# Dividing the last three block products of a Strassen-Winograd MLP layer once more

## The chip, the cores and the metric

The kernel runs on one core of a Trainium2 chip. The metric is the device time of one execution in microseconds. Before the change it was 453.57 us, the median of three runs (452.7 to 453.67).

## The reference

The input is 32 sequences of 128 tokens with 512 features, in float32. A conditional block works on it as 8 long sequences of 1024 tokens: a first residual branch (an MLP from 512 to 512 features in two directions, on masked tokens alone), and a second one, an MLP from 512 to 1024 and back to 512 on all tokens. The change touches the second branch only. Cut to that:

```python
ff_ada = silu(t) @ ffada_w + ffada_b
shift_mlp, scale_mlp, gate_mlp = split(ff_ada, 3)
ff_norm = layernorm(x) * (1 + scale_mlp) + shift_mlp
h = gelu(ff_norm @ ff_w1 + ff_b1)          # 512 -> 1024, tanh form
out = x + gate_mlp * (h @ ff_w2 + ff_b2)   # 1024 -> 512
```

## The kernel before, in words

The second branch goes over the 4096 tokens in four rounds, called pairs (p = 0 to 3). A pair holds 8 sequences of 128 tokens, 4 on each of two sides. Both layers are computed by Winograd's form of Strassen's method: a matrix product is divided into 2 x 2 blocks, and 7 block products P1 to P7 take the place of 8. With S1 to S4 the four sums of blocks of the left operand (S1 = a21 + a22, S2 = S1 - a11, S3 = a11 - a21, S4 = a12 - S2), the products are P1 = a11 b11, P2 = a12 b21, P3 = S4 b22, P4 = a22 T4, P5 = S1 T1, P6 = S2 T2, P7 = S3 T3, with T1 to T4 four such differences of the weights. The result's blocks are P1 + P2 (block 11), P1 + P6 + P5 + P3 (12), P1 + P6 + P7 + P4 (21) and P1 + P6 + P7 + P5 (22).

**The first layer** (class FirstProduct) is divided twice: seven streams of seven inner products. Its matmuls have line 1123, and its results are the two hidden tiles ha and hb of the pair. The streams run in pairs ("windows"); while one window's products run on TensorE, VectorE and GpSimd add what its results need (on VectorE lines 1148, 1153, 1167 and the sums of the next streams' tokens, `token_sums`, lines 1051 to 1061; on GpSimd lines 1174, 1203, 1207), and ScalarE copies results out of PSUM (L1181) or applies gelu.

**The second layer** (class SecondProduct) is divided once, for two halves of the pair's tokens, U (c = 0) and V (c = 1), apart. A block product is 8 matmul calls (2 tiles of 128 tokens by 4 of features) of 256 columns each, all at line 1310; the profile has two records for a call. Each token half has two PSUM banks, e and a, that products are added onto one after the other: P5, P2, P3 onto e; P1, P6, P7, P4 onto a. The order is a list, and steps of the list carry further work ("fills") that is issued behind them:

```python
ORDER = "P1U P5U P1V P5V P2U P6U P2V P6V P3U P7U P3V P7V P4U P4V".split()
```

What stands behind a product: after P5, ScalarE keeps e as `p5` (L1016) and VectorE makes S2; after P2, VectorE multiplies block 11 with the gate, adds it to the residual x (`finish`, lines 1284 and 1286), and makes the fourth block in place in ha's second half; after P6, e becomes a + p5 (L1334), to which P3 is added; after P3 block 12 is finished; after P7 block 22 is made (L1340) and finished; after P4 block 21, and the side is stored. The third block is made in place in hb's first half (L1274).

**The next pair** is prepared by fills: its rows are normalised (L934) and turned on VectorE (L1481), carried into feature rows by DMAs, scaled and shifted by ScalarE (`scaled`, 16 activations a side, L944), and cut into blocks by four sums of 1024 elements on VectorE (`TokenBlocks.one`, L991, called `begin` 1 to 4). Then the next pair's first stream's products P5, P1 stand behind step 11 (P7V), P2 and P6 behind step 12 (P4U) of the list, and the sums of weights for its streams are loaded on the SyncE queue (`load_weights`, L1069, tile tw). In pair 0 the second layer's T1 to T4 are made as well (`combine`, by VectorE). In the last pair P4V is split in two halves that are finished apart (L1324). A window of the first layer follows: the next pair's (stream 2) P5 and P1, (stream 1) P3 and P7, (stream 2) P2 and so on; the seed of a stream's e bank for stream 2 is line 1167, that of P3 of stream 1 is line 1148.

Of the kernel before, what the change touches and what calls it, by code (L numbers as in the profile page):

```python
# [22 lines left out]
def kernel(  # L23
# [883 lines left out]
    ORDER = "P1U P5U P1V P5V P2U P6U P2V P6V P3U P7U P3V P7V P4U P4V".split()  # L907
# [64 lines left out]
    class TokenBlocks:  # L972


        def __init__(self, p, xT):
            hk = KC // 2
            self.xa, self.xb = xT
            self.s12 = sp.tile([P, 2 * hk, G * S], F32, tag="s12", name=f"s12_{p}")
            self.s4 = sp.tile([P, hk, G * S], F32, tag="s4", name=f"s4_{p}")
# [4 lines left out]
        def one(self, j):  # L984
            out, x, y, op = {
# [245 lines left out]
    class SecondProduct:  # L1231


        def __init__(self, p, h, xs):
            self.p, self.xs = p, xs
            self.ha, self.hb = h
            self.banks, self.p5, self.gate = {}, {}, {}
# [54 lines left out]
        def step(self, step, late=False):  # L1292
            p, ha, hb, s1, w = self.p, self.ha, self.hb, self.s1, fw2_of.of
            hh = HC // 2
            product, n = ORDER[step][:2], ORDER[step][2]
            c = "UV".index(n)
            tok = self.cols[c]
            e, a = self.banks[c]
            bank = bank_of(product, (e, a))
            src = {  # L1300
                "P1": ha[:, :hh, tok], "P2": ha[:, hh:, tok], "P3": ha[:, hh:, tok],
                "P4": hb[:, hh:, tok], "P5": s1[c], "P6": s1[c], "P7": hb[:, :hh, tok],
            }[product]
            last = p == NP - 1 and step == len(ORDER) - 1
            for i in range(2):
                part = bank[:, ts(i, D // 2)]
                if last:
                    part = ps_t.tile([P, 512], F32, tag="tr", name=f"last_{i}")[:, : D // 2]
                for k in range(hh):
                    nc.tensor.matmul(  # L1310
                        part,
                        src[:, k, ts(i, P)],
                        w[product][:, k, :],
                        start=(last and k == 0),
# [3 lines left out]
                if last:  # L1318

                    t = tp.tile([P, D // 2], F32, tag="t", name=f"t_last_{i}")  # L1320
                    gate = self.gate[1][:, 2 * c + i, : D // 2]
                    nc.vector.tensor_tensor(t, part, gate, ALU.mult)
                    xt = self.xs[1][c][:, i, : D // 2]
                    nc.vector.tensor_tensor(xt, xt, t, ALU.add)  # L1324
                    nc.sync.dma_start(out[(2 * p + 1) * G + 2 * c + i, :, : D // 2], xt)
# [3 lines left out]
            elif product == "P2":  # L1329
                self.finish(c, 0, 0, e)  # L1330

                nc.vector.tensor_tensor(ha[:, hh:, tok], ha[:, hh:, tok], s1[c], ALU.subtract)
            elif product == "P6":
                nc.vector.tensor_tensor(e, a, self.p5[c], ALU.add)  # L1334
            elif product == "P3":
                self.finish(c, 0, 1, e)
                self.store(c, 0)
            elif product == "P7":
                t = tp.tile([P, 512], F32, tag="t", name=f"c22_o{p}_{c}")
                nc.vector.tensor_tensor(t, a, self.p5[c], ALU.add)  # L1340
                self.finish(c, 1, 1, t)
                if p == NP - 1 and n == "V":
                    b = (2 * p + 1) * G + 2 * c
                    nc.sync.dma_start(
                        out[b : b + 2, :, D // 2 :].rearrange("b s d -> s b d"),
                        self.xs[1][c][:, :, D // 2 :],
                    )
                    self.finish(c, 1, 0, a)
            elif product == "P4" and not last:
                self.finish(c, 1, 0, a)  # L1350
                self.store(c, 1)
# [55 lines left out]
    gp = straight.enter_context(tc.tile_pool(name="gp", bufs=1))  # L1407
    now = FirstProduct(0, of_x[0].cut(), of_w)
# [25 lines left out]
    for p in range(NP):  # L1434
# [93 lines left out]
        fill = {5: [lambda: second.third_block(0)], 7: [lambda: second.third_block(1)]}  # L1528
# [4 lines left out]
        if p == 0:  # L1533
            put(2, fw2_of.combine, 2)
            put(6, fw2_of.combine, 3)
        if more_pairs:
# [3 lines left out]
            for k in range(KC):  # L1540
                put(4 + k // 2, lambda k: scaled(2 * (p + 1), xT[0], k), k)
                put(7 + k // 2, lambda k: scaled(2 * (p + 1) + 1, xT[1], k), k)
                if k == 1:
                    put(4, to_feature_rows, 1, nc.sync, nc.sync, nc.sync, nc.scalar)
# [6 lines left out]
            put(8, begin, 1)  # L1551
            put(9, begin, 2)
            put(9, begin, 3)
            put(10, begin, 4)
# [6 lines left out]
            put(10, next_product)  # L1561
            put(11, lambda: nxt["p"].do(1, "P5", "P1"))
            for n in range(4):
                put(11 + n // 2, lambda n: nxt["p"].token_sums(1, n), n)
            if p + 2 < NP:
                x_of[p + 2] = [[], []]
                put(11, lambda: x_of[p + 2][0].extend(load_side(p + 2, 0)))
            put(12, lambda: nxt["p"].do(1, "P2", "P6"))
            put(13, lambda: nxt["p"].load_weights(2))
# [130 lines left out]
```

## Time and profile before

| | us |
|---|---|
| median of three runs | 453.57 |
| lowest, highest | 452.7, 453.67 |
| the profiled execution: span | 451.7 |
| median less that span | 1.9 |

| engine | busy us | share of the span |
|---|---|---|
| TensorE (PE) | 444.0 | 98% |
| VectorE (DVE) | 334.5 | 74% |
| ScalarE (ACT) | 177.9 | 39% |
| GpSimd (POOL) | 158.4 | 35% |

The profile is of one execution. Its span runs from the first to the last instruction. A row of the timeline has the start of an instruction or a group in us, its duration, the engine, the line in the code, the operation, the output tile, the inputs and the shape, then how many instructions it stands for, and in brackets the idle time before it with what ended that. A row of the groups has line, engine, operation and tiles, the number of instructions, then the busy us and the mean ns of one, then the idle time before them. Numbers of buffers are left out of the tiles' names there.

### The profile page before, as it was taken

Reading aid. Unit: us, or ns where it says so; the run is one execution under the profiler, and the core shown is the slowest. Engines: PE = TensorE matmul, PEld = TensorE weight load, DVE = VectorE, ACT = ScalarE, POOL = GpSimd, SP = SyncE. Lnnn points to the kernel's source line nnn. Section 1 sums busy time; section 2 is a strip of 40 time slices with the busy share of each in tenths; the row PEclk is TensorE's granted clock in tenths of the full one; section 3 lists DMA queues with packets and bytes.
Section 4 is the critical chain, followed back from the end, with each engine's and each line's share of the span. In section 5 each row is a group of like instructions: output and inputs, shape, how many; then the busy total and the mean of one; then the engine's idle time right before and its main releaser. Section 6 shows DMA issues by size and latency. Waiting matters only on the chain.

```text
span 451.7 us, 6204 instructions
## 1 busy us (share of the span) xinstructions
PE 444.0 (98%) x2147; PEld 370.2 (82%) x2147; DVE 334.5 (74%) x573; ACT 177.9 (39%) x389; POOL 158.4 (35%) x154
## 2 busy tenths in 40 slices
PE   8999999999999999999999999999999999999995
PEld 3884675688888888888888888888888888888884
DVE  5797788877799759977895689878956885434645
ACT  3123116353651551536526415464265244642000
POOL 4211470089770000897600007977000027560000
PEclk9999999999999999999999999999999999999999
DMA  6999449857327717741396177512971534122022
GB/s 250 372 399 408 177 65 308 284 187 229 129 97 168 108 49 268 235 138 36 105 177 93 46 267 230 141 38 86 189 99 47 176 128 129 35 93 95 0 94 96
DMA packets 85440, 70.84 MB, mean 157 GB/s; under 512 B 63396, under 2 KB 64508, under 8 KB 84382
## 3 DMA queue, kind: packets, MB, share of 16 engines
q1 hardware_dynamic: 64270, 57.76, 42.3%
q0 software_dynamic: 4160, 10.54, 6.9%
q10 hardware_dynamic: 16976, 2.11, 3.9%
q8 instruction: 18, 0.29, 0.3%
q14 instruction: 16, 0.13, 0.1%
HBM read 56.71 MB, written 13.70 MB: 156 GB/s over the span
## 4 chain that ended last, share of the span: by engine, by line
PE 84%; DMA 8%; DVE 3%; issue 2%; POOL 1%; SPq 0%; POOLq 0%
PE a_o L1310 24%; PE a_m L1123 21%; PE e_o L1310 18%; PE e_m L1123 16%; DMA fw<-in_L_cond_ff_w_dram 3%; PE po_s L222 3%; DMA w<-in_L_cond_bwd_w_dram 3%; DMA x_wide<-t_s 2%; DMA x<-x_wide,slot_i 1%; DVE t L403 1%; PE last L1310 1%; PE a_m_alone L1123 1%; POOL x L819 1%; PE ptr L950 0%; PE pl_s L255 0%
## 5 line engine op out<-in xcount | busy, mean ns | idle before, releaser
L1174 POOL TENSOR_TENSOR ha<-p_m,ha 128x512 f32<-128x512 f32 x20 | 25.8, 1292 | 176.0 <-ACT ha L1181 166.1
L1310 PE MATMUL e_o<-fw,ha 128*128 128x256 f32 x256 | 57.9, 379 | 0.0
L944 ACT ACTIVATE xT<-xT,modT 128x128 f32<-128x128 f32 x112 | 44.0, 480 | 28.1 <-DMA xT<-xn 28.1
L1310 PE MATMUL a_o<-t,hb 128*128 128x256 f32 x240 | 54.1, 379 | 0.0
L1310 PEld LDWEIGHTS e_o<-fw,ha 128*128 128x128 f32 x256 | 48.6, 190 | 6.6
L1310 PEld LDWEIGHTS a_o<-t,hb 128*128 128x128 f32 x240 | 45.6, 190 | 6.2
L1085 ACT ACTIVATE hb<-hb,biasT 128x256 f32<-128x256 f32 x64 | 29.0, 500 | 28.3 <-POOL hb L1207 16.1
L1137 ACT COPY p_m<-e_m 128x512 f32<-128x512 f32 x27 | 15.8, 586 | 51.6 <-PE e_m L1123 51.6
L890 POOL DMA_INDIRECT x<-x_rows,slot_i x24 | 27.2, 1135 | 6.2 <-issue 5.4
L1174 POOL TENSOR_TENSOR hb<-p_m,hb 128x512 f32<-128x512 f32 x20 | 29.2, 1460 | 0.3
L1310 PE MATMUL a_o<-fw,ha 128*128 128x256 f32 x128 | 28.9, 379 | 0.0
L1310 PE MATMUL a_o<-t,s 128*128 128x256 f32 x128 | 28.9, 379 | 0.0
L1310 PE MATMUL e_o<-fw,s 128*128 128x256 f32 x128 | 28.9, 379 | 0.0
L222 PE MATMUL po_s<-w,h_s 128*128 128x512 f32 x64 | 28.4, 594 | 0.0
L1181 ACT COPY ha<-e_m 128x512 f32<-128x512 f32 x32 | 18.5, 579 | 24.8 <-PE e_m L1123 24.4
L1310 PEld LDWEIGHTS a_o<-fw,ha 128*128 128x128 f32 x128 | 24.3, 190 | 3.3
L1310 PEld LDWEIGHTS a_o<-t,s 128*128 128x128 f32 x128 | 24.3, 190 | 3.3
L1310 PEld LDWEIGHTS e_o<-fw,s 128*128 128x128 f32 x128 | 24.3, 190 | 3.3
L1148 DVE TENSOR_TENSOR e_m<-a_m,ha 128x512 f32<-128x512 f32 x20 | 14.0, 698 | 17.0 <-POOL ha L1174 7.6
L1085 ACT ACTIVATE ha<-e_m,biasT 128x256 f32<-128x256 f32 x48 | 20.0, 468 | 14.4 <-PE e_m L1123 14.4
L1123 PE MATMUL a_m<-xT,tw 128*128 128x256 f32 x96 | 24.7, 380 | 0.0
L1123 PE MATMUL e_m<-s,fw 128*128 128x256 f32 x92 | 23.7, 380 | 0.0
(234 smaller groups left out, 894.1 us busy)
## 6 DMA issues: line engine op xcount, KB each, us to landing
x<-in_x_dram SPq DMA_DIRECT2D x16, 512.0 KB, 5.9
tw<-t_rows SPq DMA_DIRECT2D x16, 512.0 KB, 4.3
gate<-gate_rows POOLq DMA_DIRECT2D x8, 1024.0 KB, 5.1
out_dram<-x SPq DMA_DIRECT2D x15, 512.0 KB, 4.7
tw<-t_rows SPq DMA_DIRECT2D x16, 384.0 KB, 3.9
xT<-xn SPq DMA_DIRECT2D x80, 64.0 KB, 2.7
ada_f<-in_L_cond_ffada_w_dram SPq DMA_DIRECT2D x4, 768.0 KB, 14.8
ada_a<-in_L_cond_ada_w_dram SPq DMA_DIRECT2D x4, 512.0 KB, 3.6
```

The costliest lines, as they stand in the source:

```text
L222: nc.tensor.matmul(po, h[f][:, ts(i, P)], w[:, f, :], start=(f == 0 and seeded is None), stop=(f == HC - 1), skip_group_check=seeded is no ...
L403: engine.tensor_tensor(out, x, y, ALU.subtract)
L819: nc.gpsimd.indirect_dma_start(out=raw[i // 2][:, i % 2], out_offset=None, in_=x1_wide[:slots], in_offset=bass.IndirectOffsetOnAxis(ap=slo ...
L890: nc.gpsimd.indirect_dma_start(out=xs[i // G][i % G // 2][:, i % 2], out_offset=None, in_=x1_rows, in_offset=bass.IndirectOffsetOnAxis(ap= ...
L944: nc.scalar.activation(out, src, AF.Identity, bias=shift, scale=scale)
L1085: nc.scalar.activation(dst[:, n], src[:, n], AF.Gelu_apprx_tanh, bias=biasT[:, f : f + 1])
L1123: nc.tensor.matmul(bank[:, ts(n, QT)], self.w_block(j, product)[:, ts(n, P)], self.x_block(j, product), start=(product in ("P1", "P5") and ...
L1137: nc.scalar.copy(p5, e)
L1148: nc.vector.tensor_tensor(e, a, p5, add)
L1174: nc.gpsimd.tensor_tensor(self.place(RESULT[j], c), self.p5[j], other, ALU.add)
L1181: nc.scalar.copy(self.place(RESULT[j], c), src)
L1310: nc.tensor.matmul(part, src[:, k, ts(i, P)], w[product][:, k, :], start=(last and k == 0), stop=True, skip_group_check=True,)
```

## The change

P3, P7 and P4 of the second layer are no longer 8 calls of 256 columns for each token half. Each is done for U and V together and divided once more by the same method into seven inner products p1 to p7 (class Inner): left blocks of 2 feature tiles by 256 tokens, right blocks of 2 feature tiles by 128 columns, so an inner product is 4 calls of 128 columns. The three are written A (P3), B (P7) and C (P4) below.

- *Their sums of the left operand* (512 elements a lane each): sums 1, 2 and 3 of A, B and C are on GpSimd, sum 4 on VectorE. All three share one tile (`si`) for sums 1 and 2; sum 3 and sum 4 are made in place in ha or hb.
- *Inner products apart*: p5 has a bank of its own, and p1, p6, p7 are added onto another; ScalarE copies what stands in the bank after each into a tile d (tag xn) of parts.
- *Inner products direct*: p2, p3 and p4 are added onto the banks e (A) or a (B and C) of U and V.
- *Fives and joins* on GpSimd: `with_five` adds the p5 part to a half of d (256 elements), and `join` adds the parts of one token half (512 elements) to p5 of the layer (A: d + p5 in d; B: p5 + d in p5; C: d + B's d in d).
- *On VectorE* e's seed takes A's parts in place of p5 (`seed_third`), block 22 takes p5 with B's parts, block 21 gets one more addition (`sum_of` with C's parts) for U and for V. In the last pair, V's block 21 is done in place with C's p4 in two halves (`last_quarters`).
- *The inner weights*: twelve subtractions of 256 elements on GpSimd in pair 0 (`inner_weights`), and the layer's combine(3) moves from VectorE to GpSimd.
- *Fills*: they are now named by inner products. The scaling of the next pair's second side is issued in halves behind p6A to p7B, `begin` 1 to 4 behind p7B, p4A, p1C and p6C; the next pair's P5 and P1 of the first stream behind p4B, P2 and P6 behind p3C, with the loads that stood there. P6V is split around p6A.

The core of the diff:

```diff
-    ORDER = "P1U P5U P1V P5V P2U P6U P2V P6V P3U P7U P3V P7V P4U P4V".split()
+    ORDER = "P1U P5U P1V P5V P2U P2V P6U".split()
+    INNER = ("P3", "P7", "P4")
...
+        def join(self, product, c, engine):
+            d = self.inner[product].d[:, c]
+            if product == "P3":
+                engine.tensor_tensor(d, d, self.five(c), ALU.add)
+            elif product == "P7":
+                engine.tensor_tensor(self.five(c), self.five(c), d, ALU.add)
+            else:
+                engine.tensor_tensor(d, d, self.inner["P7"].d[:, c], ALU.add)
...
+        def sum(self, j, engine):
+            (a11, a12), (a21, a22) = self.x
+            s1, s2 = self.s
+            out, x, y, op = {
+                1: (s1, a21, a22, ALU.add),
+                2: (s2, s1, a11, ALU.subtract),
+                3: (a21, a11, a21, ALU.subtract),
+                4: (a11, a12, s2, ALU.subtract),
+            }[j]
+            engine.tensor_tensor(out, x, y, op)
...
+        def apart(self, q):
...
+            nc.scalar.copy(self.d[:, c, :, ts(n, P)], view)
+
+        def with_five(self, c, engine):
+            d = self.d
+            other = d[:, 1, :, P:] if c == 0 else d[:, 1, :, :P]
+            engine.tensor_tensor(d[:, c, :, P:], d[:, c, :, P:], other, ALU.add)
...
         if p == 0:
+            put(2, inner_weights, "P7")
             put(2, fw2_of.combine, 2)
-            put(6, fw2_of.combine, 3)
+            put(3, lambda: fw2_of.combine(3, engine=nc.gpsimd))
+            put(3, inner_weights, "P3")
+            put(4, inner_weights, "P4")
...
+        put(5, sums, PA, 1, 2, 3)
...
+        run("p5A", lambda: inner[PA].apart("p5"))
+        sums(PB, 1)
+        run("p1A", lambda: inner[PA].apart("p1"))
+        sums(PA, 4, engine=nc.vector)
+        second.multiply("P6V", (0,))
+        run("p6A", lambda: inner[PA].apart("p6"))
+        inner[PA].with_five(0, nc.gpsimd)
+        second.multiply("P6V", (1,))
+        run("p7A", lambda: inner[PA].apart("p7"))
+        second.join(PA, 0, nc.gpsimd)
+        second.seed_third(0)
+        inner[PA].with_five(1, nc.gpsimd)
+        second.join(PA, 1, nc.gpsimd)
+        second.seed_third(1)
+        sums(PB, 2)
+        inner[PB].apart("p5")
+        run("p1B", lambda: inner[PB].apart("p1"))
+        sums(PB, 3)
+        sums(PB, 4, engine=nc.vector)
+        second.direct(PA, "p2")
+        run("p6B", lambda: inner[PB].apart("p6"))
+        sums(PC, 1)
+        second.direct(PA, "p3")
+        second.finish_third(0)
+        run("p7B", lambda: inner[PB].apart("p7"))
+        sums(PC, 2)
+        inner[PB].with_five(0, nc.gpsimd)
+        second.join(PB, 0, nc.gpsimd)
+        sums(PC, 3)
+        run("p4A", lambda: second.direct(PA, "p4"))
+        second.finish_third(1)
+        inner[PB].with_five(1, nc.gpsimd)
+        second.join(PB, 1, nc.gpsimd)
+        inner[PC].apart("p5")
+        run("p1C", lambda: inner[PC].apart("p1"))
+        sums(PC, 4, engine=nc.vector)
+        second.direct(PB, "p2")
+        run("p6C", lambda: inner[PC].apart("p6"))
+        inner[PC].with_five(0, nc.gpsimd)
+        second.join(PC, 0, nc.gpsimd)
+        second.direct(PB, "p3")
+        second.finish_22(0)
+        inner[PC].apart("p7")
+        inner[PC].with_five(1, nc.gpsimd)
+        second.join(PC, 1, nc.gpsimd)
+        run("p4B", lambda: second.direct(PB, "p4"))
+        second.finish_22(1)
+        run("p2C", lambda: second.direct(PC, "p2"))
+        second.direct(PC, "p3")
+        second.finish_21(0)
```

In the listings below a row has the line in the code, the instruction, the output tile, the inputs and the shape; x8 or x4 is the number of calls. A name's first number is the pair's (a bank e_o1_0 is pair 1's of U; fw2 and t_2 are the second layer's weights and their differences).

TensorE in pair 1, before: after V's P6 (row one) come U's and V's P3 and P7; the products follow one another, and the next pair's first stream (e_m2_1, a_m2_1) stands between them.

```order
L1310 MATMUL a_o1_1_1790<-t_2_314,s1_1_1505 128x256 x8
L1310 MATMUL e_o1_0_1731<-fw2_312,ha_1_1432 128x256 x8
L1310 MATMUL a_o1_0_1732<-t_2_314,hb_1_1433 128x256 x8
L1310 MATMUL e_o1_1_1789<-fw2_312,ha_1_1432 128x256 x8
L1310 MATMUL a_o1_1_1790<-t_2_314,hb_1_1433 128x256 x8
L1123 MATMUL e_m2_1_2023<-s12_2_1974,fw1_311 128x256 x2
```

TensorE in pair 1, now: the inner products of A (five_1_P3, one_1_P3) and B (five_1_P7, one_1_P7), with A's p2 and p3 direct onto U's bank e.

```order
L1453 MATMUL five_1_P3_2034<-fw2_312,si_1_2015 128x128 x4
L1453 MATMUL one_1_P3_2041<-fw2_312,ha_1_1515 128x128 x4
L1395 MATMUL a_o1_1_1887<-t_2_314,s1_1_1602 128x256 x4
L1453 MATMUL one_1_P3_2041<-t_1_313,si_1_2015 128x128 x4
L1395 MATMUL a_o1_1_1887<-t_2_314,s1_1_1602 128x256 x4
L1453 MATMUL one_1_P3_2041<-t_1_313,ha_1_1515 128x128 x4
L1453 MATMUL five_1_P7_2083<-t_2_314,si_1_2015 128x128 x4
L1453 MATMUL one_1_P7_2089<-t_2_314,hb_1_1516 128x128 x4
L1453 MATMUL e_o1_0_1828<-fw2_312,ha_1_1515 128x128 x4
L1453 MATMUL one_1_P7_2089<-inner_more_892,si_1_2015 128x128 x4
L1453 MATMUL e_o1_0_1828<-fw2_312,ha_1_1515 128x128 x4
```

Between A's p7 (the sixth row) and B's p6 (the tenth, which reads `si`) stand three inner products.

GpSimd in pair 1, before: between the loads of the gate and the next pair's first layer it has nothing.

```order
L928 TENSOR_TENSOR rstd_3_1_2082<-ve_3_1_2338,half_134 128x4
L901 DMA gate_2_0_2341<-gate_rows_699 128x2048
L901 DMA gate_2_1_2389<-gate_rows_699 128x2048
L1174 TENSOR_TENSOR ha_3_2578<-p5_m3_2_2648,ha_3_2578 128x2x256
L1174 TENSOR_TENSOR hb_3_2579<-p5_m3_2_2648,hb_3_2579 128x2x256
```

GpSimd in pair 1, now (L1444 is a sum, L1476 a `with_five`, L1324 and L1326 a `join`; xn_d is the tile d, p5_o1 is p5):

```order
L901 DMA gate_1_1_1913<-gate_rows_699 128x2048
L1444 TENSOR_TENSOR si_1_2015<-ha_1_1515 128x512
L1444 TENSOR_TENSOR si_1_2015<-si_1_2015,ha_1_1515 128x512
L1444 TENSOR_TENSOR ha_1_1515<-ha_1_1515 128x2x256
L1444 TENSOR_TENSOR si_1_2015<-hb_1_1516 128x512
L1476 TENSOR_TENSOR xn_d_1_2016<-xn_d_1_2016 128x2x128
L1324 TENSOR_TENSOR xn_d_1_2016<-xn_d_1_2016,p5_o1_0_1916 128x512
L1476 TENSOR_TENSOR xn_d_1_2016<-xn_d_1_2016 128x2x128
L1324 TENSOR_TENSOR xn_d_1_2016<-xn_d_1_2016,p5_o1_1_1958 128x512
L1444 TENSOR_TENSOR si_1_2015<-si_1_2015,hb_1_1516 128x512
L1444 TENSOR_TENSOR hb_1_1516<-hb_1_1516 128x2x256
L1444 TENSOR_TENSOR si_1_2015<-hb_1_1516 128x512
```

Sum 2 of B (the tenth row) stands behind the fives and joins of both of A's halves; ten more of these instructions follow the last row shown.

VectorE at the end of pair 1, before: from the next pair's token sums (sx_2) to the two seeds (e_m2_1 and e_m2_2); t_o and x are gate and residual of block 21.

```order
L1051 TENSOR_TENSOR sx_2_2032<-xT_2_1_1889 128x512
L1051 TENSOR_TENSOR sx_2_2032<-s4_2_1975 128x256
L1148 TENSOR_TENSOR e_m2_1_2023<-a_m2_1_2024,p5_m2_1_2027 128x512
L1284 TENSOR_TENSOR t_o1_1_10_2067<-a_o1_1_1790,gate_1_1_1816 128x512
L1286 TENSOR_TENSOR x_14_899<-x_14_899,t_o1_1_10_2067 128x2x256
L1167 TENSOR_TENSOR e_m2_2_2083<-a_m2_2_2084,ha_2_2005 128x512
```

VectorE at the end of pair 1, now:

```order
L1054 TENSOR_TENSOR sx_2_2208<-xT_2_1_1986 128x512
L1054 TENSOR_TENSOR sx_2_2208<-s4_2_2170 128x256
L1343 TENSOR_TENSOR c21_o1_0_2230<-a_o1_0_1829,xn_d_1_2016 128x512
L1287 TENSOR_TENSOR t_o1_0_10_2232<-c21_o1_0_2230,gate_1_1_1913 128x512
L1289 TENSOR_TENSOR x_12_898<-x_12_898,t_o1_0_10_2232 128x2x256
L1151 TENSOR_TENSOR e_m2_1_2199<-a_m2_1_2200,p5_m2_1_2203 128x512
L1343 TENSOR_TENSOR c21_o1_1_2246<-a_o1_1_1887,xn_d_1_2016 128x512
L1287 TENSOR_TENSOR t_o1_1_10_2248<-c21_o1_1_2246,gate_1_1_1913 128x512
L1289 TENSOR_TENSOR x_14_900<-x_14_900,t_o1_1_10_2248 128x2x256
L1170 TENSOR_TENSOR e_m2_2_2264<-a_m2_2_2265,ha_2_2172 128x512
```

U's block 21 now stands between the token sums and the first seed, each half has one addition more (c21), and that addition reads d, which GpSimd's last joins write.

More of the change, by code (lines that the diff above doesn't have):

```diff
@@ L1329, in step @@
             elif product == "P2":
[L1330 to L1346, printed above, removed]
-                    )
[L1348 to L1351, printed above, removed]
+                if c == 0:
+                    self.finish(c, 0, 0, self.banks[c][0])
```

217 lines of the change are left out of this document (172 added, 45 removed).

## The prediction

> **What bounds the kernel now.** I read the page first, then the chain of waits in order of time, the groups of instructions with shapes kept apart, and the timeline of the second pair's second product (211 to 285 us), where every engine can be followed.
>
> ```profile
> PE 444.0 (98%) x2147; PEld 370.2 (82%) x2147; DVE 334.5 (74%) x573; ACT 177.9 (39%) x389; POOL 158.4 (35%) x154
> POOL 4211470089770000897600007977000027560000
> PE 84%; DMA 8%; DVE 3%; issue 2%; POOL 1%; SPq 0%; POOLq 0%
> ```
>
> TensorE is busy for 98% of the span and makes 84% of the chain that ended last. GpSimd's row has a run of zeros in each pair: those are the second products, the stage that is changed. The chain of waits shows what one block product is worth there, and two more rows bound the last pair's stage:
>
> ```profile
> 433.21 3.45 PE e_o L1310 x16
> 412.33 3.62 PE L1310 MATMUL e_o<-fw,ha 128*128 128x256 f32 x16
> 447.52 0.43 DVE L1324 TENSOR_TENSOR x<-x,t_last 128x256 f32<-128x256 f32 x1
> ```
>
> Sixteen records (each of 8 calls is recorded twice) take 3.453 us, so a record of 256 columns costs 215.8 ns, back to back. TensorE's time is the kernel's time as long as every other engine delivers ahead of it.
>
> **What TensorE saves.** A pair loses six block products, 96 records, 20.72 us, and gets 3 x 28 calls, 168 records of 128 columns. The opening has such records:
>
> ```profile
> 16.21 3.65 PEld L681 LDWEIGHTS ph_s<-xT_s,w 128*128 128x128 f32 x32 [0.35 <-issue]
> L681 PEld LDWEIGHTS ph_s<-xT_s,w 128*128 128x128 f32 x64 | 7.3, 192 | 0.4 <-issue 0.4
> ```
>
> The 32 loads start within 3.65 - 0.19 = 3.46 us, 111.6 ns apart: a load takes 192 ns, but loads overlap. So 168 x 0.1116 = 18.75 us, 1.97 us saved in a pair, **7.8 us in four**; an inner product of 8 records takes 0.893 us. The Trainium skill (TensorE: Matmul & The Clock Gate, LDWEIGHTS) gives a weight load as columns over 1.2 GHz, 107 ns for 128; by that estimate four pairs would save 11. The row is for this type and shape, and I keep it.
>
> **The first wait: B's second sum.** I call the three block products A (P3), B (P7), C (P4). GpSimd has, in this order, the fives' addition and join of A's second half, then sum 2 of B, which B's p6 reads. The first of these needs the copy of A's p7, the last inner product of A.
>
> ```profile
> L197 ACT COPY xT_s<-ptr_s 128x256 f32<-128x256 f32 x8 | 2.5, 381 | 17.6 <-PE ptr_s L194 17.6
> 230.74 3.62 PE L1310 MATMUL e_o<-fw,ha 128*128 128x256 f32 x16
> 230.94 0.58 ACT L1016 COPY p_o<-e_o 128x512 f32<-128x512 f32 x1 [3.74 <-PE e_o L1310]
> 212.42 0.58 ACT L1181 COPY ha<-e_m 128x512 f32<-128x512 f32 x1
> 213.09 1.29 POOL L1207 TENSOR_TENSOR ha<-ha 128x512 f32<-128x512 f32 x1 [2.51 <-ACT ha L1181]
> 214.46 1.27 POOL L1174 TENSOR_TENSOR ha<-p_m,ha 128x512 f32<-128x512 f32 x1
> 215.69 1.27 POOL L1207 TENSOR_TENSOR hb<-hb 128x512 f32<-128x512 f32 x1
> ```
>
> ScalarE's copy starts 0.20 after the product's end (where the next product starts) and takes 0.38; GpSimd follows 0.09 after a copy's end; its 512-wide additions stand 1.23 apart (214.46, 215.69). No row shows a 256-wide one on GpSimd: it costs between nothing and 1.23; I take half, 0.65. So B's p6 can start 0.20 + 0.38 + 0.09 + 0.65 + 1.23 + 1.23 + 0.09 = 3.87 us after A's p7, and TensorE has three inner products to fill that, 2.68. It waits 1.2 us in each pair, **4.8 us** (2.2 to 7.1 by the two ends).
>
> **The second wait: VectorE's queue at a pair's end** (the three pairs that have a next one). VectorE makes the next pair's four block sums when ScalarE has scaled the last of its rows; that scaling now stands behind the copy of B's p7.
>
> ```profile
> 246.96 6.26 ACT L944 ACTIVATE xT<-xT,modT 128x128 f32<-128x128 f32 x16 [3.15 <-DMA xT<-xn]
> 253.25 1.23 DVE L991 TENSOR_TENSOR s<-xT 128x1024 f32<-128x1024 f32 x1 [3.63 <-ACT xT L944]
> 266.71 0.69 DVE L1148 TENSOR_TENSOR e_m<-a_m,p_m 128x512 f32<-128x512 f32 x1
> 270.72 0.70 DVE L1167 TENSOR_TENSOR e_m<-a_m,ha 128x512 f32<-128x512 f32 x1 [0.38 <-PE a_m L1123]
> 272.18 1.03 PE L1123 MATMUL e_m<-xT,fw 128*128 128x256 f32 x4
> ```
>
> Before, VectorE goes from its first block sum at 253.25 to the seed of the next pair's P3 at 267.40 in 14.15 us, and the seed at 270.72 is 0.8 us ahead of the product that reads it (272.18). Now the first sum can start 0.20 + 0.38 + 2 x 0.39 + 0.09 = 1.45 us after B's p7. The same stretch holds two additions more (C's sum 4, and C's part for U): 15.5 us. Behind it stand C's part for V with gate and residual and the second seed, 4 x 0.69: 18.3. With 0.20 to TensorE that is 19.95 us, and TensorE has meanwhile 11 inner products and 8 groups of 0.863 (a quarter of 3.453), 16.7. It waits 3.2 us, **9.7 us in three pairs** (2.2 to 4 a pair, by the spacing of the additions). What is late inside: p2 of C needs the bank that VectorE reads for U, the next pair's second P1 needs U's other bank, its P3 the first seed.
>
> **The third wait: GpSimd and VectorE get in each other's way.**
>
> ```profile
> 272.19 1.27 POOL L1174 TENSOR_TENSOR ha<-p_m,ha 128x512 f32<-128x512 f32 x1 [47.35 <-ACT ha L1181]
> 272.38 0.69 DVE L1153 TENSOR_TENSOR hb<-a_m,p_m 128x512 f32<-128x512 f32 x1 [0.37 <-PE a_m L1123]
> 272.99 2.69 DVE L1055 TENSOR_TENSOR xn_sy<-sx,xT 128x512 f32<-128x512 f32 x2
> 273.42 1.71 POOL L1174 TENSOR_TENSOR hb<-p_m,hb 128x512 f32<-128x512 f32 x1
> L1055 DVE TENSOR_TENSOR xn_sy<-sx,s 128x512 f32<-128x512 f32 x4 | 2.7, 682 | 0.0
> ```
>
> Two GpSimd additions and two VectorE additions whose inputs both lie in SBUF run from 272.19 to 275.68, 3.49 us. Alone they take 2 x 1.23 and 2 x 0.6 (682 ns each, one starting before the other's end): one after the other. The VectorE addition at 272.38 reads PSUM and keeps its 0.69 beside GpSimd. The Trainium skill (SBUF — State Buffer, Who interferes with whom) says why this change is in danger: VectorE and GpSimd share a port, and a VectorE instruction with two SBUF inputs and a GpSimd instruction that reads SBUF exclude each other, the later one waiting for the whole of the other. By that rule the trace agrees; a rule by which the engines overlapped would strike this term.
>
> From the first block sum on, GpSimd still has five 512-wide and four 256-wide additions, 5 x 1.1 + 4 x 0.55 = 7.7 us of holding (1.1 is 3.49 less two additions of VectorE, halved). All of them must be done before VectorE can take C's parts, and all but a few of VectorE's 24 instructions there have two SBUF inputs. Four that read PSUM (4 x 0.66) can cover 2.6: between 5.1 and 7.7 goes into VectorE's queue; I take 6.0 as the covers won't all meet, **18 us in three pairs**.
>
> **Pair 0's weights.** GpSimd gets twelve 256-wide subtractions and one of 1024, 12 x 0.65 + 2.46 = 10.3 us, from 133.9 on, beside VectorE's normalisations.
>
> ```profile
> 133.34 0.55 POOL L901 DMA_DIRECT2D gate<-gate_rows  x1 [1.45 <-PE a_m L1123]
> 139.78 3.62 PE L1310 MATMUL e_o<-fw,ha 128*128 128x256 f32 x16
> 144.49 0.71 DVE L1481 STREAM_TRANSPOSE xn<-xn 128x512 f32<-128x512 f32 x1
> 218.73 1.57 DVE L934 TENSOR_SCALAR xn<-x,mv,rstd 128x512 f32<-128x512 f32 x1
> 220.97 0.52 DVE L934 TENSOR_SCALAR xn<-x,mv,rstd 128x512 f32<-128x512 f32 x1
> ```
>
> A normalisation took 1.57 instead of 0.52 beside a GpSimd addition. Up to 145.2 VectorE has six of them and four two-input operations: ten waits of some 0.4, 4 us, so it is free 9.4 us after U's P2 (139.78). Then follow finish, U's and V's fourth block and A's sum 1: 9.4 + 1.4 + 1.2 + 1.2 + 1.27 + 0.2 = 14.7, and A's p5 was due after three block products, 10.4: **4.3 us** (0 to 7).
>
> **The last pair's end** has no next pair, but GpSimd's queue sets it. Sum 2 of B ends where B's p6 starts, 4 x 3.453 + 7 x 0.893 + 1.2 = 21.3 us after U's P2. Then come eight 512-wide and four 256-wide additions, 12.4 us, and eight two-input operations of VectorE between them, 8 x 0.55 = 4.4 (0 if they pass each other): 38.1. VectorE's final addition, half of the last product and four half-size operations bring it to 40.8. Before it was 447.95 - 412.33 = 35.6. So the last pair loses 5.2; beyond its share of the two terms above (-1.97 + 1.2) that is **6.0 us**.
>
> At nothing I cost: the twelve copies a pair on ScalarE (0.38 each, 39% busy; cover is gone where the scaling's transfer lands late: at 246.96, 16.2 us after U's P2, A's p7 copy is done just when p1 of B needs its bank, and each us later costs one); and the SyncE queue, where the loads of weight sums stand behind U's and V's stores, which come later with VectorE.
>
> ```profile
> tw<-t_rows SPq DMA_DIRECT2D x16, 512.0 KB, 4.3
> 260.65 1.30 SPq L1069 DMA_DIRECT2D tw<-t_rows  x2
> 274.77 1.03 PE L1123 MATMUL e_m<-sx,tw 128*128 128x256 f32 x4
> ```
>
> Issued at 260.65 and read at 274.77, with 4.3 to land, they have 9.8 us to give.
>
> **The sum**, against the profiled execution (span 451.7, and 1.9 around it to the median of 453.57): -7.8 + 4.8 + 9.7 + 18.0 + 4.3 + 6.0 = +35.0, so 488.6 us.
>
> **Rivals.** *VectorE and GpSimd pass each other in this stage*: the third term, the weights' 4.3 and 4.4 of the last pair go: +8.3, 462 us. For it: most GpSimd additions in the trace show 1.27 beside busy VectorE; against it: those neighbours read PSUM or one input. *The sums stay hidden*, faster: the place is B's p6. If a 512-wide GpSimd addition took 0.77 us or less (0.77 x 2.5 + 0.76 = 2.68), GpSimd would keep up, VectorE would begin earlier, and TensorE's 7.8 would be kept: 445.8. The 1.27 of each row speaks against it. *The change's matmuls don't get shorter*: if loads did not overlap (192 ns), TensorE would need 32.3 us a pair for the 18.75, +54 at most with much of the waiting inside it, some 500; row L681 speaks against it.
>
> **Chances.** Forecast (both engines in turn) 0.68; they pass each other 0.17; loads 0.03; hidden 0.10; costs and gains cancel 0.02. The forecast's own range, all bounds at one end, is 475 to 502; to hold 8 in 10, mine reaches down to 460 for the first rival and up to 502. A measurement of this kernel tells 0.2%, 0.9 us, from no change: faster 0.10, same 0.02, slower 0.88.
>
> **What would show it.** Right: TensorE's share well under 98%, with waits of about 1.2 us at B's p6 for GpSimd in all four pairs; additions on both engines in the second half of a pair longer than 1.27 and 0.69; at a pair's end p2 of C and the next pair's P3 waiting for VectorE; GpSimd's last join 38 us after U's P2 in the last pair. Records of 128 columns should be 112 ns apart. Wrong: GpSimd additions at 1.27 and VectorE's at 0.69 side by side, or a full TensorE row; then the second rival holds.

## The result, and the profile after

The changed kernel took 496.79 us (median of four runs, 496.03 to 498.46) against 453.2 for the kernel before on the same chip: a ratio of 1.0965, with an interval of 1.0943 to 1.0987. The forecast was 488.6 (460 to 502). The profiled execution has a span of 494.2 us, 42.5 more than before.

The page of the changed kernel, its lines on the engines, GpSimd's slices, the granted clock and the chain:

```profile
PE 451.2 (91%) x2435; PEld 379.1 (77%) x2435; DVE 385.5 (78%) x592; ACT 194.5 (39%) x437; POOL 290.9 (59%) x251
POOL 4221530697877891897149928973389328531892
PEclk9999999999998999999999979999999899999995
PE 63%; DVE 19%; issue 7%; POOL 6%; DMA 2%; SPq 2%; ACT 1%; DVEq 0%; POOLq 0%
```

TensorE fell from 98% of the span to 91, and from 84% of the chain to 63; VectorE rose from 3% to 19. GpSimd's run of zeros is filled. The view of TensorE's waits says for whom (us in total, times, longest):

```profile
PE a_o L1453 <- DVE c_o L1343: 8.4, 4, 2.4
PE a_o L1453 <- DVE t_last L1377: 6.8, 2, 6.4
PE one_P L1453 <- POOL hb L1444: 5.5, 4, 1.7
PE one_P L1453 <- POOL si L1444: 5.2, 4, 1.4
PE five_P L1453 <- POOL si L1444: 3.9, 1, 3.9
PE e_m L1126 <- DVE e_m L1151: 2.8, 3, 0.9
PE a_m L1126 <- DVE c_o L1343: 2.8, 3, 1.0
PE e_m L1126 <- DVE e_m L1170: 1.3, 2, 0.7
```

Before, TensorE had no wait in these stages. From the top: C's p2 (and once p4) waits until VectorE has read the bank for block 22; C's p4 in the last pair waits for VectorE; C's p7 waits for C's sum 3, B's p6 for B's sum 2, and pair 0's first p5 for A's sum 1; then come three places of the next pair. Together they are 36.7 us.

TensorE in the second pair, where each kind stands once:

```profile
255.22 1.05 PE L1453 MATMUL five_P<-fw,si 128*128 128x128 f32 x8
256.11 1.06 PE L1453 MATMUL one_P<-fw,ha 128*128 128x128 f32 x8
...
266.71 1.16 PE L1453 MATMUL one_P<-inner_more,si 128*128 128x128 f32 x8 [1.32 <-POOL si L1444]
...
276.71 1.16 PE L1453 MATMUL one_P<-fw,hb 128*128 128x128 f32 x8 [1.70 <-POOL hb L1444]
...
282.87 3.66 PE L1453 MATMUL a_o<-t,hb 128*128 128x128 f32 x16 [2.38 <-DVE c_o L1343]
...
290.95 1.13 PE L1126 MATMUL a_m<-xT,fw 128*128 128x256 f32 x4 [0.93 <-DVE c_o L1343]
293.01 2.02 PE L1126 MATMUL e_m<-s,fw 128*128 128x256 f32 x4 [0.93 <-DVE e_m L1151]
```

An inner product without a wait takes 0.89 us (255.22 to 256.11), as forecast. The two products at 282.87 take 3.5 us instead of 1.79, which is the clock (below). GpSimd and VectorE in the same pair, a few rows of each:

```profile
261.27 0.72 POOL L1476 TENSOR_TENSOR xn_d<-xn_d 128x256 f32<-128x256 f32 x1
262.07 1.27 POOL L1324 TENSOR_TENSOR xn_d<-xn_d,p_o 128x512 f32<-128x512 f32 x1
...
271.07 1.18 POOL L1476 TENSOR_TENSOR xn_d<-xn_d 128x256 f32<-128x256 f32 x1
272.32 2.13 POOL L1326 TENSOR_TENSOR p_o<-p_o,xn_d 128x512 f32<-128x512 f32 x1
```

```profile
271.58 1.74 DVE L994 TENSOR_TENSOR s<-xT 128x1024 f32<-128x1024 f32 x1
273.36 2.18 DVE L994 TENSOR_TENSOR s<-s,xT 128x1024 f32<-128x1024 f32 x1
...
294.92 0.69 DVE L1170 TENSOR_TENSOR e_m<-a_m,ha 128x512 f32<-128x512 f32 x1
```

While VectorE is idle (until 263.37) GpSimd's additions take 0.72 and 1.27; beside VectorE's finishing and block sums, from 271 on, they take 1.18 and 2.13, and VectorE's block sums 1.74 and 2.18 where they took 1.23. That one waits for the other is what these lengths suggest; the experiments test it. From VectorE's first block sum to the end of its second seed it is 295.61 - 271.58 = 24.03 us; the forecast's terms were 18.3 for the instructions and 6.0 for GpSimd, 24.3.

### The profile page after: what moved, and what is told of

Its sections match the earlier page's. It is cut to its first block, busy times and chain, and to the rows that moved or that the text cites. A ratio compares the mean times of both kernels' runs of the same rounds, so it can differ in the third digit from the quotient of the medians.

```text
span 494.2 us, 7054 instructions
## 1 busy us (share of the span) xinstructions
PE 451.2 (91%) x2435; PEld 379.1 (77%) x2435; DVE 385.5 (78%) x592; ACT 194.5 (39%) x437; POOL 290.9 (59%) x251
## 3 DMA queue, kind: packets, MB, share of 16 engines
q1 hardware_dynamic: 64542, 57.76, 38.1%
## 4 chain that ended last, share of the span: by engine, by line
PE 63%; DVE 19%; issue 7%; POOL 6%; DMA 2%; SPq 2%; ACT 1%; DVEq 0%; POOLq 0%
PE a_m L1126 16%; PE e_m L1126 13%; PE e_o L1395 8%; PE po_s L222 6%; PE a_o L1395 5%; PE ph_s L205 4%; DVE t_o L1287 3%; DVE s L994 2%; PE a_o L1453 2%; POOL si L1444 2%; DMA xT<-xn 2%; SPq L962 2%; DVE sx L1054 2%; DVE c_o L1343 2%; PE ph_s L681 2%
## 5 line engine op out<-in xcount | busy, mean ns | idle before, releaser
L945 ACT ACTIVATE xT<-xT,modT 128x128 f32<-128x128 f32 x112 | 45.8, 483 | 25.4 <-DMA xT<-xn 25.3
L1444 POOL TENSOR_TENSOR si<-ha 128x512 f32<-128x512 f32 x4 | 5.1, 1265 | 44.4 <-DVE ha L1406 43.2
L1289 DVE TENSOR_TENSOR x<-x,t_o 128x512 f32<-128x512 f32 x31 | 29.7, 958 | 1.1
L1453 PE MATMUL a_o<-t,hb 128*128 128x128 f32 x160 | 22.8, 296 | 7.1 <-DVE c_o L1343 7.1
L1395 PE MATMUL e_o<-fw,ha 128*128 128x256 f32 x128 | 28.3, 379 | 0.0
L1470 ACT COPY xn_d<-one_P 128x256 f32<-128x256 f32 x36 | 13.3, 368 | 37.7 <-PE one_P L1453 37.7
L1126 PE MATMUL e_m<-s,fw 128*128 128x256 f32 x92 | 25.1, 397 | 2.8 <-DVE e_m L1151 2.8
L1453 PEld LDWEIGHTS a_o<-t,hb 128*128 128x128 f32 x160 | 21.2, 209 | 8.3 <-DVE c_o L1343 8.3
L1395 PEld LDWEIGHTS a_o<-fw,ha 128*128 128x128 f32 x128 | 24.3, 190 | 3.3
```

Source lines behind the costliest of these rows:

```text
L945: nc.scalar.activation(out, src, AF.Identity, bias=shift, scale=scale)
L1126: nc.tensor.matmul(bank[:, ts(n, QT)], self.w_block(j, product)[:, ts(n, P)], self.x_block(j, product), start=(product in ("P1", "P5") and ...
L1395: nc.tensor.matmul(bank[:, ts(i, D // 2)], src[:, k, ts(i, P)], w[product][:, k, :], start=False, stop=True, skip_group_check=True,)
L1453: nc.tensor.matmul(out[:, i], src[:, k, ts(i, P)], self.w[q][:, k, :], start=(start and i == 0 and k == 0), stop=True, skip_group_check=True,)
```

## The experiments

Ratios are against the kernel before on the same chip.

**GpSimd's additions left out.** First try:

```diff
-                inner[product].sum(j, engine)
+                if engine is nc.vector:
+                    inner[product].sum(j, engine)
...
+            return          # in with_five and in join
...
-                "p5": self.s[0], "p6": self.s[1], "p7": a21
+                "p5": a11, "p6": a11, "p7": a21
```

> The changed kernel without GpSimd's additions in the second products: sums 1 to 3, fives and joins are left out in all pairs (p5 and p6 read a block of the hidden tile in their place); the inner weights, VectorE's sum 4 and its second addition for block 21 stay. By the theory of the prediction (GpSimd's length makes B's p6 wait, and GpSimd's SBUF accesses hold VectorE up at a pair's end) what is left is -7.8 of TensorE, at most 9.7 of VectorE's own longer queue, about 5 of pair 0's weights and 1 to 3 at the last pair's end: 453 to 464 us. If VectorE's queue is late by its own length and GpSimd's work merely runs beside it, only the waits that the trace puts down to GpSimd go (B's p6 and C's p7, 12 us): about 485 us.

Measured: 475.21 us, ratio 1.0502 (1.0472 to 1.0533). Between the two, and the reason is a fault of the experiment: TensorE waits at C's p6 for VectorE's sum 4, which overwrites the block that p6 was made to read.

```profile
268.59 1.13 PE L1450 MATMUL one_P<-fw,hb 128*128 128x128 f32 x8 [3.36 <-DVE hb L1441]
```

It decides nothing. (VectorE's sum 4 reads a21 in place of sum 2, here and in the next run.) Again, with `"p5": a22, "p6": a22`:

> As left_out (GpSimd's sums, fives and joins of the second products left out), but p5 and p6 read the block that no sum writes: in left_out they read the block that VectorE's sum 4 overwrites, so that p6 waited for it (3.4 us at C's p6 in three pairs). The prediction's terms without GpSimd: -7.8 of TensorE, 9.7 of VectorE's queue, 5 of pair 0's weights, 1 to 3 at the last pair's end: 460 to 464 us; with a slower clock behind the waits up to 3 more. If VectorE's queue is late by much more than its own length, it stays at 470 us or above.

Measured: 464.63 us, ratio 1.0272 (1.0247 to 1.0296), 0.6 above the 460 to 464. VectorE and TensorE at the second pair's end:

```profile
258.45 1.23 DVE L994 TENSOR_TENSOR s<-xT 128x1024 f32<-128x1024 f32 x1 [0.69 <-ACT xT L945]
...
276.01 0.69 DVE L1170 TENSOR_TENSOR e_m<-a_m,ha 128x512 f32<-128x512 f32 x1
```

```profile
272.04 1.13 PE L1126 MATMUL a_m<-xT,fw 128*128 128x256 f32 x4 [0.70 <-DVE c_o L1344]
274.10 1.13 PE L1126 MATMUL e_m<-s,fw 128*128 128x256 f32 x4 [0.93 <-DVE e_m L1151]
276.75 1.13 PE L1126 MATMUL e_m<-xT,fw 128*128 128x256 f32 x4 [0.66 <-DVE e_m L1170]
```

VectorE's stretch is 276.70 - 258.45 = 18.25 us: the 18.3 of the forecast, undisturbed. TensorE waits 2.29 us for it and loses some 0.27 more at each wait (below), 3.1: the forecast had 3.2. GpSimd's additions thus cost 496.8 - 464.6 = 32.2 us; the three terms put down to GpSimd (4.8, 18.0, 6.0) made 28.8. The two are not quite the same sum: without the additions the clock records show half speed only from 454.38 to the end, so the 32.2 hold up to 6 us of slower clock that no term had (below), and part of the 6.0 stays as a wait of TensorE for VectorE.

**All additions on VectorE** (`nc.gpsimd` replaced by `nc.vector` in sums, fives and joins):

> The changed kernel with all its sums, fives and joins on VectorE and none on GpSimd (the inner weights stay on GpSimd). VectorE gets 9 sums and 6 joins of 0.6 and 6 fives of 0.35 more in a pair, 16.5 us less the 5.4 before the first block sum, 11.1 us at a pair's end at most. By the theory of turns GpSimd's additions hold VectorE up by more than that (42 us from 253.3 to 295.5, of which some 23 are VectorE's own at undisturbed lengths), so the time falls: 5 to 8 us in each of three pairs, 465 to 480 us. If the engines pass each other and VectorE's queue is the bound, the time rises by up to 11 us in three pairs: 505 to 530 us.

Measured: 490.46 us, 1.0812 (1.0794 to 1.0831): faster than the changed kernel, but 10 us above the 465 to 480 that were forecast.

```profile
271.17 1.23 DVE L994 TENSOR_TENSOR s<-xT 128x1024 f32<-128x1024 f32 x1 [0.67 <-ACT xT L945]
...
294.24 0.69 DVE L1170 TENSOR_TENSOR e_m<-a_m,ha 128x512 f32<-128x512 f32 x1
```

VectorE's stretch is 23.76 us, no shorter than the 24.03. Every instruction has its undisturbed length, and the ten additions that moved into it make up for what GpSimd had held it: 23.76 - 18.25 = 5.5 of work against 24.03 - 18.25 = 5.8 of holding. My 42 less 23 had counted what lies ahead of the stretch too. The sign speaks for turns, since engines that pass each other would have given over 505; the size was wrong, so this run alone decides little.

**Two additions to the kernel before**, which leave its computation as it is:

```diff
+            def added():
+                for _ in range(8):
+                    nc.gpsimd.tensor_tensor(scratch, xT[1][:, 3], scratch, ALU.subtract)
+            put(8, added)
```

> The kernel before with eight more additions of 512 elements on GpSimd in each of three pairs, which read SBUF and whose result nobody reads; they start when ScalarE has scaled the last rows of the next pair, as VectorE's first block sum does, and nothing waits for them. If the engines take turns at SBUF, VectorE loses 8 x 1.1 = 8.8 us there, less its lead of 0.8 and what its instructions on PSUM cover (1 to 2): 5 to 8 us a pair, 468 to 477 us. If they pass each other, 453 us.

and with one such addition and `for _ in range(16): nc.gpsimd.memset(scratch, 0.0)` behind it:

> As before_adds, but one such addition and then sixteen GpSimd instructions that set the same 512 elements to zero: they write SBUF and read nothing. If it is the reading of SBUF by both that excludes, only the one addition costs, 453 to 455 us; if any use of SBUF by GpSimd excludes, about as much as the eight additions, for as long as these take.

Measured: 465.49 us, 1.0274 (1.0257 to 1.0291), for the additions, and 452.77, 1.0001 (0.9992 to 1.0011), for the sets. GpSimd and VectorE with the additions:

```profile
258.13 15.65 POOL L1550 TENSOR_TENSOR scratch<-xT,scratch 128x512 f32<-128x512 f32 x8 [28.38 <-ACT xT L944]
280.29 1.76 POOL L1174 TENSOR_TENSOR ha<-p_m,ha 128x512 f32<-128x512 f32 x1 [6.51 <-ACT ha L1181]
```

```profile
258.08 1.23 DVE L991 TENSOR_TENSOR s<-xT 128x1024 f32<-128x1024 f32 x1 [3.54 <-ACT xT L944]
...
262.58 2.29 DVE L991 TENSOR_TENSOR s<-s,xT 128x1024 f32<-128x1024 f32 x1
...
279.64 0.69 DVE L1167 TENSOR_TENSOR e_m<-a_m,ha 128x512 f32<-128x512 f32 x1
```

and with the sets:

```profile
255.99 9.26 POOL L1551 MEMSET scratch<- 128x512 f32 x16
```

```profile
257.12 1.22 DVE L991 TENSOR_TENSOR s<-s,xT 128x1024 f32<-128x1024 f32 x1
```

Nobody waits for these GpSimd instructions, yet eight additions cost 12.7 us in three pairs, 4.2 each: a little under the 5 to 8. They take 15.65 us in place of 8 x 1.23, VectorE's second block sum 2.29 in place of 1.22. Nor do they delay GpSimd's own next work: it had been idle for 6.51 us when that began (280.29), and it waited for ScalarE. Sixteen sets run 9.26 us beside VectorE and cost nothing; VectorE's second block sum keeps its 1.22 there. So it is not GpSimd's being busy that holds VectorE up; what the additions do and the sets don't is read SBUF. The Trainium skill (SBUF — State Buffer, Who interferes with whom) says so: a VectorE instruction with two SBUF inputs contends with a GpSimd instruction that reads SBUF, not with one that only writes it. By both runs the trace agrees.

**B's sum 2 first**:

```diff
         second.seed_third(0)
+        sums(PB, 2)
         inner[PA].with_five(1, nc.gpsimd)
         second.join(PA, 1, nc.gpsimd)
         second.seed_third(1)
-        sums(PB, 2)
```

> The changed kernel with B's sum 2 ahead of the five and the join of A's second half on GpSimd, where it no longer stands behind the copy of A's p7. If B's p6 wait is a loss by itself, 1.3 to 1.5 us go in each of four pairs: 491 us. If it is given back at the pair's end, where GpSimd and VectorE fill the time between them, 495 to 497 us.

Measured: 497.07 us, 1.096 (1.093 to 1.0989): nothing gained. B's p6 no longer waits, but:

```profile
272.94 1.74 DVE L994 TENSOR_TENSOR s<-xT 128x1024 f32<-128x1024 f32 x1
```

```profile
269.31 1.16 PE L1453 MATMUL one_P<-inner_more,hb 128*128 128x128 f32 x8 [0.63 <-POOL hb L1444]
...
278.07 1.38 PE L1453 MATMUL one_P<-fw,hb 128*128 128x128 f32 x8 [2.25 <-POOL hb L1444]
```

B's p7 waits 0.63 for sum 3, and C's p7 2.25 where it was 1.70. The queue is as long as it was: A's p5 starts at 256.64 here and at 255.22 in the changed kernel, 1.42 apart, and VectorE's first block sum at 272.94 and 271.58, 1.36 apart. It stands behind B's sum 4 on VectorE, which waits for GpSimd's sums of B in either order.

**Pair 0's weights left out** (the loop of `nc.gpsimd.tensor_tensor(o, x, y, ALU.subtract)` in `inner_weights` removed):

> The changed kernel without the twelve subtractions of the inner weights in pair 0 (they are left out, blocks of the weights are read in their place; the sum of 1024 elements stays on GpSimd). By the prediction 4.3 us of pair 0's wait go, 492.5 us; with the slower clock that the trace shows behind that wait (3.41 us at half speed, 1.5 us) 491. If VectorE's longer queue in pair 0 comes from elsewhere, no change: 497 us.

Measured: 492.61 us, 1.0877 (1.0859 to 1.0895), 4.2 less than the changed kernel, as forecast. But the wait does not go whole:

```profile
150.71 1.16 PE L1453 MATMUL five_P<-fw,si 128*128 128x128 f32 x8 [1.25 <-POOL si L1444]
```

Pair 0's p5 still waits 1.25 of its 3.90 us. From U's P1 of pair 0 to that of pair 1 it is 103.0 us in place of 105.7, so 2.8 us less in the profiled execution, and its whole span is 3.3 us shorter (490.9 against 494.2). That the medians differ by 4.2, so close to the term's 4.3, is in part luck.

**Idle matmuls in TensorE's waits**:

```diff
+        def busy(self, which, calls):
+            out = self.banks[which][:, 2 * P : 3 * P]
+            t = self.w["p1"][:, 0, :]
+            for _ in range(calls):
+                nc.tensor.matmul(out, t, t, start=False, stop=True, skip_group_check=True)
```

> The changed kernel with idle matmuls of 128 columns, whose results nobody reads, in three of TensorE's waits: 14 ahead of pair 0's p5 of A, 8 ahead of C's p2 in the three pairs with a next one, 24 ahead of C's p4 in the last pair, each less than the wait there. If the half clock of 3.41 us that follows these waits in the trace comes from TensorE's idleness, it stays at full clock and the slow stretches of 1.5 to 1.8 us (pair 0's p5, the three pair ends) and the 0.9 at the end go, as far as VectorE does not set the end there: 490 to 494 us. If the clock falls for another reason, 497 us as before.

Measured: 494.95 us, 1.0934 (1.0913 to 1.0956), 1 us above the forecast's range. The stretches at the second pair's end, of the changed kernel and with the idle matmuls (columns: the stretch, its length, then busy time and instructions of TensorE, its loads, VectorE, ScalarE and GpSimd, the granted clock, DMA share, GB/s):

```profile
279.46:282.87 3.41, 1.03 (x5) 0.57 (x3) 3.27 (x4) 1.16 (x2) 3.33 (x3) 1.00 0.98 305
282.87:286.28 3.41, 3.41 (x16) 3.41 (x17) 3.38 (x3) 0.00 (x0) 3.20 (x3) 0.50 0.75 288
```

```profile
282.90:286.20 3.30, 3.30 (x23) 3.13 (x24) 3.27 (x3) 0.38 (x1) 3.11 (x3) 1.00 0.80 298
```

The clock stays at full speed where TensorE is kept busy, so its idleness was the cause. Before the end it fell twice, in pair 0 (from 165.95 and from 183.01), each time behind 3.41 us in which TensorE was idle for 1.75 and 2.31 us all the same. But only 1.8 us came back: C's p4, which had no wait in this pair, now waits for VectorE:

```profile
287.89 1.16 PE L1458 MATMUL a_o<-fw,hb 128*128 128x128 f32 x8 [1.30 <-DVE c_o L1343]
```

**The last pair's p4 not behind VectorE**:

```diff
-            nc.vector.tensor_tensor(a, a, d, ALU.add)
-            self.gated_quarter(a, 1, slice(0, 2))
             t, w = "p4", self.inner["P4"]
-            for i in range(2):
-                w.multiply(t, a[:, :, :P], False, (i,))
-                self.gated_quarter(a, 0, slice(i, i + 1))
+            w.multiply(t, a[:, :, :P], False)
+            for n in (1, 0):
+                cols = ts(n, P)
+                nc.vector.tensor_tensor(d[:, :, cols], a[:, :, cols], d[:, :, cols], ALU.add)
+                self.gated_quarter(d, n, slice(0, 2))
```

> The changed kernel, where in the last pair C's p4 is added onto V's bank as in the other pairs, and VectorE adds the parts behind it: TensorE no longer waits for VectorE's addition in place (6.4 us in the trace) and for the quarter's gate (0.4 us). If that order made the last pair's end longer than forecast, the two half products with their waits go (487.04 to 490.2 us of the trace) and VectorE's additions alone are left: 2 to 3 us less, 494 to 495 us. If VectorE's queue alone sets the end, within 1 us of 497.

Measured: 494.62 us, 1.0935 (1.0918 to 1.0951), 2.2 less than the changed kernel, as forecast.

**Only A divided once more**, in three versions. The first:

> Only the first of the three (P3, called A) is divided once more; P7 and P4 are as in the kernel before. GpSimd has A's sums 1 to 3, right behind the fourth blocks; sum 4, fives and joins are on VectorE ahead of the first block sum, where VectorE was idle for 3.6 us before; VectorE also takes the last four of the 16 scalings, so that ScalarE's three copies more don't delay the first block sum. TensorE saves 2 x 3.453 - 7 x 0.893 = 0.66 us a pair, 2.6 us. If what counts is whether GpSimd and VectorE get in each other's way where VectorE is late (a pair's second half), all of it stays: 450 to 451.5 us. If any work put between two products comes back as a wait, 453 to 457 us.

Measured: 460.48 us, 1.0162 (1.0148 to 1.0176), slower than either expectation. TensorE waited for a ScalarE copy that stood behind scalings, which had waited for a DMA:

```profile
250.47 1.13 PE L1464 MATMUL one_P<-inner_more,si 128*128 128x128 f32 x8 [1.17 <-ACT xn_d L1481]
```

> As a_only, with A's sums 1 to 3 on VectorE too, so that GpSimd has nothing in the second products but pair 0's four subtractions, and with ScalarE's work put in the order in which it is waited for: the copies of A's p1 and p6 stood behind scalings that waited for a DMA, and p6 waited 1.2 to 1.7 us for them in three pairs; the third scaling of the first side now follows p1's copy, the fourth goes to VectorE, and one of the second side's goes ahead of p7's copy, so that the first block sum starts earlier. The three waits of a_only for the copies (4.7 us) and those in the next window (4.4 us) should go: 451 to 453 us. If VectorE's queue is late by the 2.6 + 1.8 us of additions that it gets, 455 us or more.

Measured: 453.96 us, 1.0024 (1.0012 to 1.0036), 1 us above the 451 to 453. Most waits are gone; left are one of 0.7 us in a next window and pair 0's two, where VectorE is fuller:

```profile
151.70 1.13 PE L1464 MATMUL five_P<-fw,si 128*128 128x128 f32 x8 [1.32 <-DVE si L1455]
...
159.76 3.72 PE L1406 MATMUL a_o<-t,hb 128*128 128x256 f32 x16 [0.80 <-DVE e_o L1333]
```

> As a_only_2, but in pair 0 the P3 of both halves is not divided; the four subtractions for its weights stand on GpSimd behind it. The 2.4 us of waits that a_only_2 has in pair 0 go (1.48 and 0.96), and with them one of four savings of 0.66; ScalarE scales the second side's rows behind p7's copy, so that p7's copy doesn't wait for a DMA. Left are 3 x 0.66 = 2.0 us saved and at most the 0.8 of a wait in the next window: 451 to 452 us, a little faster than before. If VectorE's additions before the first block sum have used up its lead, 453 us or more.

Measured: 455.09 us, 1.0049 (1.0031 to 1.0067): not faster. A wait of 0.7 us stays in pair 0, and another took the place of those that went, behind a chain whose start is a gather on GpSimd that waits for the load of x:

```profile
294.27 1.13 PE L1126 MATMUL a_m<-xn_sy,tw 128*128 128x256 f32 x4 [1.60 <-DVE hb L1156]
```

```profile
283.86 0.99 POOL L890 DMA_INDIRECT x<-x_rows,slot_i  x1 [3.04 <-DMA x<-in_x_dram]
```

Why that load comes later than before (there the gathers at 281.02 and 282.56 have no such wait) was not tried. No version that was run beats the kernel before.

## Why the prediction came out right, and which steps were off

- **TensorE's saving**, -7.8: right. An inner product takes 0.89 us, so the rival in which loads do not overlap falls.
- **B's p6**, +4.8: the waits are there, 5.2 us in four pairs. As a term of its own it is wrong: with the wait taken away the time stayed (B's sum 2 first), because GpSimd's queue is late at the next product all the same, and VectorE begins its block sums no earlier. The sum let TensorE's lateness at B's p6 and VectorE's at the pair's end add up, where GpSimd's queue sets both, and had no term for C's p7 (5.5), which is the same lateness further on.
- **VectorE's queue**, +9.7, and **the turns**, +18.0: right in mechanism and in the length of the stretch (18.25 and 5.8 against 18.3 and 6.0). The rival that the engines pass each other falls by the eight additions to the kernel before, and the one that the sums stay hidden falls by GpSimd's 1.27. That the two are what TensorE loses at a pair's end is right to 3 us. From U's P1 of one pair to that of the next it was 105.7, 101.1 and 100.4 us (starts at 122.67, 228.41, 329.53 and 429.88) against 90.9, 90.9 and 90.7, so 14.8, 10.2 and 9.7 longer. Add the 1.97 saved, and take off B's p6 (1.4 to 1.6 by the starts of products) and in pair 0 its first wait with the slow clock behind it (5.5): about 10 are left in each pair, 30 against 27.7. Part of the difference is that VectorE's first block sum starts 2.1 us after the end of B's p7 (269.49, 271.58), not 1.45, as it stands behind VectorE's finishing of block 12. Of VectorE's 25 instructions from there to the second seed seven read PSUM, and two of these run while GpSimd still adds (up to 286.15), where the prediction counted 24 and four; its 6.0 for the turns met 5.8 all the same.
- **Pair 0's weights**, +4.3: right in mechanism, and near in size: 3.9 us of waiting, of which 2.65 go without them (3.90 less 1.25), and 2.8 us of the pair. The way there is the forecast's too: VectorE's fourth blocks come late, and take 3.41 us for two where they take 2 x 1.22 undisturbed.

```profile
148.72 3.41 DVE L1406 TENSOR_TENSOR ha<-ha,s 128x1024 f32<-128x1024 f32 x2
```

- **The last pair's end**, +6.0: mis-sized. GpSimd's last join ended 38.4 us after U's P2 (446.29), against 38.1 forecast, but VectorE's last addition 44.2 after it, against 40.8.

```profile
483.05 1.59 POOL L1328 TENSOR_TENSOR xn_d<-xn_d 128x512 f32<-128x512 f32 x1
```

```profile
485.83 0.69 DVE L1364 TENSOR_TENSOR a_o<-a_o,xn_d 128x512 f32<-128x512 f32 x1
...
490.23 0.29 DVE L1379 TENSOR_TENSOR x<-x,t_last 128x128 f32<-128x128 f32 x1
```

The step that failed is "VectorE's final addition, half of the last product and four half-size operations", put at 2.7 us behind GpSimd's last join; it took 5.9. VectorE is still finishing U's block 21 when the join ends (484.64) and adds V's parts into the bank only at 485.83; C's p4 may be added onto the bank only behind that, so two half products and VectorE's steps follow one after the other, at half clock (from 484.25 on). That wait stands without GpSimd's additions too, and with p4 not behind VectorE 2.2 of the 3.4 come back.

```profile
454.98 1.23 PE L1450 MATMUL a_o<-fw,hb 128*128 128x128 f32 x4 [3.84 <-DVE t_last L1378]
```

(That row is of the kernel without GpSimd's additions, second try.)

- **Not forecast**: the clock and the cost of a wait itself. Of the 42.5 us of span, 36.7 are waits and -7.8 the saving; the rest is 13.6. By the rows some 7 of it are the products that run at half clock, and some 6 what the 23 waits cost beyond their shown length, 0.27 each (both in the last section).

The whole was right in its mechanism and short in its size: 8.2 us above the forecast. In the profile the three pairs with a next one are 34.7 us longer against 29.7 by the terms, and the last pair is 8.5 us longer against 5.2. That the miss is not larger is in part luck, as the 4.8 that the sum had as a term of its own stands in the place of the clock and the waits' own cost, which it lacked.

## What to carry to other kernels

A kernel whose TensorE is full has its slack in other engines' queues, and a saving on TensorE is worth what those queues can still take: here 7.8 us were saved for 21 additions more on GpSimd and 5 on VectorE in each pair. GpSimd was no spare VectorE for additions from SBUF to SBUF: beside eight of them three of VectorE's four block sums took 2.29 us in place of 1.22, so first look where VectorE is idle. And a wait that is removed is a gain only if the queue behind it was not late anyway: find the engine that stays busy through the stretch, and compare its length before and after.

## What the runs showed of the hardware

**The clock falls by windows.** In the changed kernel the clock records show half speed from 153.16, 282.87, 293.11 and 385.26 us, 3.41 us each, and from 484.25 to the end: the differences from the first are 38, 41, 68 and 97 times 3.413. Over the fourteen kernels of this case, a window of that grid at full clock in which TensorE was idle for 2.05 us or more was always followed by half clock, one with less than 1.75 never; between them, both occur. The window ahead of 293.11 held two waits of 0.93, 1.86 us. The Trainium skill (TensorE: Matmul & The Clock Gate, Part 1: The HAM clock gate) has the window of 3413 ns, and that it runs free; the trace agrees with both. The Trainium skill asks there for a whole idle window before the clock falls; here 1.86 us of 3.41 could be enough.

**A wait costs more than it shows.** At 266.71 the wait is given as 1.32 us. By starts of inner products (264.33 for the one before, 267.70 for the next) the pair of them took 3.37 in place of 1.79: 0.27 more than the wait. At 276.71 it is the same (273.96 to 277.71 is 3.75, with a wait of 1.70). A product's record is 1.06 long although the next starts 0.89 after it, so a wait that is counted from the record's end misses 0.17; the product behind the wait then takes 1.16, 0.10 more.

**GpSimd's 256-wide addition** takes 0.72 us, more than half of the 1.27 for twice as much; I had taken 0.65.
